# Deeper buffers between the engines of a selective scan, with its sums issued one step later

## The chip, the cores and the metric

The kernel runs on one core of a Trainium2 chip. A core has TensorE (PE), VectorE (DVE), ScalarE (ACT), GpSimd (POOL) and SyncE (SP); each takes its instructions in the order in which the program gives them to it, and waits at the head of its queue when an instruction needs something that is not there yet. SP's queue holds DMAs only. The metric is the device time of one execution in microseconds (us).

## The reference

Eight images of 64 channels by 64 x 64 go through four layers: attention over all 4096 positions with a depthwise convolution (layer 0), two blocks of window attention with MLPs (layer 1), a convolution by generated filters (layer 2), and a state-space layer (layer 3). The change concerns the scan of layer 3 most. Per image it has 128 channels, 16 states and four directions over the 4096 positions:

```
def step(h, inp):
    u_t, dt_t, B_t, C_t = inp
    h = h * jnp.exp(dt_t[..., None] * A) + dt_t[..., None] * B_t[:, :, None, :] * u_t[..., None]
    return (h, jnp.einsum('bkcn,bkn->bkc', h, C_t))
_, ys = jax.lax.scan(step, h0, (u, dt, Bl, Cl))
...
y = out_y[:, 0] + inv[:, 0] + wh + invwh
y = _ln(y, outnorm_g, outnorm_b, LN_EPS) * jax.nn.silu(z)
return jnp.einsum('bhwd,cd->bhwc', y, outproj_w) + outproj_b
```

Everything is float32.

## The kernel before

Images go in pairs, four pairs in all. For a pair, `front` does layers 0 to 2 and the inputs of layer 3, `scans` does the scan, and `back` the rest of layer 3. While the scans of pair p run, the back of pair p-1 and then the front of pair p+1 run beside them: `scans` takes a piece of that work (a Python generator that yields at each piece) after each scan step, as many as a fixed share of the whole asks for. In the last pair's scans there is only back work beside. The front of the first pair, with layer 0 of the second, comes ahead of all scans and takes about 2190 us.

A unit of the scan is one image, one direction and 512 positions; a pair has 64 units. A unit has eight steps, so there are 512 steps to a pair and 2048 in all. A step handles two states of all 128 channels: each partition holds one state of one channel, and the two halves of the channels lie side by side in tiles of 128 x 2 x 512.

A step i consists of these instructions:

- `fetch` (L1732): rows of B and of C are read from memory and spread over the partitions, by SP. B and C have four tiles each. B is fetched three steps ahead and C two.
- `products` (L1740): POOL multiplies B by dt times x, two steps ahead, into a tile `v`. There are six such tiles.
- `step`: ACT computes the two exponentials `dad` in PSUM (L1762), DVE scans (L1765) into a tile `h`, or into the PSUM tile itself, and ACT copies the last value of each scan to `carry` (L1773). Even steps have an `h` of two halves, odd steps of one, and there is one tile of each kind.
- The product with C overwrites `v`. `own` says how many of the two halves DVE multiplies (L1779) instead of POOL (L1776 for both halves, L1779 for one): 0 in even and 1 in odd steps, one more during the attention of layer 0, and 1, 1, 1, 2 in the last pair.
- `sums` (L1791): two matmuls with the constant matrix `fold` add the two states of each channel into the PSUM tile `yd`, which collects the eight steps of a unit. After the eighth, DVE adds `yd` into `Y` (L1803, L1805 or, for the fourth direction, L1808 into the tile `xs`, which SP stores as `ys`).

`inputs` prepares the unit after the next one: SP loads `xs` (L1705, two tiles), PE and ACT compute dt from it (L1708 to L1716), and SP spreads it over the partitions as `du` (L1719) and writes the rows of B and C to memory (L1725). The loop of `scans` writes all this in this order:

```
self.fetch(i + 3, steps[i + 3], 0)
self.fetch(i + 2, steps[i + 2], 1)
self.products(i + 2, steps[i + 2])
self.step(i, steps[i])
if i:
    self.sums(i - 1, steps[i - 1], steps[i]["w"])
while done < cost * (i + 1) / (n - LEAD):
    done += next(beside, cost)
if i % 8 == 1: self.inputs(self.units[i // 8 + 1])
```

A scheduler then puts each engine's instructions in order by its own estimate of when they are ready, so that several products can stand ahead of their step. `steps[i]["w"]` is the first product with C of step i; the sum is kept behind it in that estimate, which adds no wait on the chip.

Large tiles of the work beside the scans are slabs of 128 x 4356 floats, of which there are three; smaller ones come from pools that each part opens for itself, `w1a` and `w1m` for window attention and the MLP, `w2` for layer 2, `w4` and `w5` for back.

Of the kernel before, what the change touches and what calls it, by code (L numbers as in the profile page):

```python
# [9 lines left out]
F32 = mybir.dt.float32  # L10
# [7 lines left out]
P = 128  # L18
CH = 512
# [3 lines left out]
TAPS = 9  # L23
DI, NST, RNK, KDIR = 128, 16, 4, 4
TD = 512
NTD = L // TD
LEAD = 24
AHEAD = 0.8
# [60 lines left out]
def _pack(w):  # L89
# [105 lines left out]
    put("drT", f["dtproj_w"].transpose(2, 0, 1))  # L195
    al = f["A_logs"].reshape(KDIR, 2, 64, NST // 2, 2)
    put("alogs", al.transpose(2, 4, 0, 3, 1).reshape(P, KDIR, NST))
    put("fold", np.repeat(eye, 2, axis=0))
    dtT = f["dtproj_w"].transpose(2, 0, 1)
# [960 lines left out]
class _Direct:  # L1160
# [66 lines left out]
    def img(t):  # L1227
        return t.rearrange("p (h w) -> p h w", w=64)

    def memory(self, name, shape=(P, L)):  # L1230
        return self.dram.tile(list(shape), F32, name=name, tag=name)
# [128 lines left out]
    def layer1(self, X):  # L1360
        nc, tc, w, net = self.nc, self.tc, self.w, self.net
        with tc.tile_pool(name="w1n", bufs=2) as wk:
            for c in range(NCH):
                x = X[:, c * CH : (c + 1) * CH]
                pc, sd = self.normed(wk, lambda pc: [(pc, x)], w["cen64"], w["avg64"], net.eps[:, 0:1])
                nc.vector.scalar_tensor_tensor(x, pc, w["pe_g"], sd, ALU.mult, ALU.mult)
                nc.scalar.activation(x, x, AF.Identity, bias=w["pe_b"])
                yield 6
        for i in range(2):
            with tc.tile_pool(name="w1a", bufs=2) as wk:  # L1370
                now = self.window_head(i, 0, X, wk)
                for wy in range(8):

                    def ahead(wy=wy):
                        return self.window_head(i, wy + 1, X, wk) if wy < 7 else None

                    now = yield from self.window_row(i, wy, X, now, ahead, wk)
            with tc.tile_pool(name="w1m", bufs=2) as wk:
                yield from self.mlp(i, X, wk)

    def window_head(self, i, wy, X, wk):
# [16 lines left out]
        nc.tensor.matmul(pq, lhsT=w[f"qw{i}"], rhs=H, start=True, stop=True)  # L1398
        qx = wk.tile([P, 8, 4, 64], F32, name="w_qx", tag="w_qx", bufs=1)
        for s in range(4):  # L1400
# [21 lines left out]
    def window_row(self, i, wy, X, now, ahead, wk):  # L1422
# [6 lines left out]
        def scores(x):  # L1429

            es = []
            ss = [self.bank(f"w_s{g}", (P, 2, 4, 64)) for g in range(2)]
            for j in range(2):
                for g in range(2):
                    for im in range(2):
                        rows = slice(64 * im + 32 * g, 64 * im + 32 * g + 32)
                        nc.tensor.matmul(  # L1437
                            ss[g][half[im], j],
                            lhsT=K[rows, 64 * (x + j) : 64 * (x + j) + 64],
                            rhs=qx[rows, x + j],  # L1440
                            start=True,
                            stop=True,
                        )
            kinds = [2 * (wy == 7) + (x + j == 7) if shift else 0 for j in range(2)]
            for g in range(2):
                hs = slice(4 * g, 4 * g + 4)
                e = wk.tile([P, 2, 4, 64], F32, name="w_e", tag="w_e", bufs=4)
                b = bias[:, 0, hs].unsqueeze(1).to_broadcast([P, 2, 4, 64])
                nc.vector.tensor_tensor(e, ss[g], b, ALU.add)  # L1449
                for j in range(2):  # L1450
                    if kinds[j]:
                        m = net.smask[:, kinds[j] : kinds[j] + 1].to_broadcast([P, 4, 64])
                        nc.vector.tensor_tensor(e[:, j], e[:, j], m, ALU.add)
                nc.scalar.activation(e, e, AF.Exp)  # L1454
                es.append(e)
            return es
# [61 lines left out]
    def mlp(self, i, X, wk):  # L1518
        nc, w, net, half = self.nc, self.w, self.net, self.HALF
        gelus = []  # L1520
        for c in range(NCH):
            x = X[:, c * CH : (c + 1) * CH]
            pc, sd = self.normed(wk, lambda pc: [(pc, x)], w["cen64"], w["avg64"], net.eps[:, 0:1])
            H = wk.tile([P, CH], F32, name="m_h", tag="m_h")
            nc.vector.scalar_tensor_tensor(H, pc, w[f"norm2_g{i}"], sd, ALU.mult, ALU.mult)
            hid = []
            for im in range(2):
                ph = self.bank("ph")
                nc.tensor.matmul(ph, lhsT=w[f"f1w{i}"][half[im], :], rhs=H[half[im]], start=True, stop=True)
                h = wk.tile([P, CH], F32, name="hid", tag="hid", bufs=4)  # L1530
                g = nc.scalar.activation(h, ph, AF.Gelu, bias=net.bf1[:, i : i + 1])
                hid.append(h)
# [7 lines left out]
    def layer2(self, X):  # L1540
        nc, tc, w, net = self.nc, self.tc, self.w, self.net
        XP = self.padded("XP")
        for c in range(NCH):
            nc.scalar.activation(self.rows(XP, c), self.img(X[:, c * CH : (c + 1) * CH]), AF.Copy)
            yield 1
        nr = 2 * TAPS
        with tc.tile_pool(name="w2", bufs=2) as wk:
            net.load(wk, (5,))
            cf = net.channel_filters(X, wk, self.pf, "f")
            for c in range(NCH):  # L1550
# [18 lines left out]
                for t in range(TAPS):  # L1569
# [89 lines left out]
    def scans(self, p, beside, cost):  # L1659
# [16 lines left out]
        for i in range(-3, n):  # L1676
# [22 lines left out]
    def inputs(self, u):  # L1699
# [9 lines left out]
        one = wk.tile([P, 2, TD], F32, name="du1", tag="du1", bufs=1)  # L1709
        du = u["du"] = wk.tile([P, 2, 2, TD], F32, name="du", tag="du")  # L1710
        nc.scalar.activation(
# [4 lines left out]
        nc.scalar.activation(one[:, 0], pd, AF.Copy)  # L1716
        for g in range(2):
            src = one[self.HALF[g]].rearrange("c q t -> c (q t)").unsqueeze(1).to_broadcast([64, 2, 2 * TD])
            nc.sync.dma_start(du[:, g].rearrange("p q t -> p (q t)"), src)  # L1719
# [18 lines left out]
    def products(self, i, st):  # L1738
        v = st["v"] = self.sw.tile([P, 2, TD], F32, name="vd", tag="v", bufs=6)
        self.nc.gpsimd.tensor_tensor(v, self.twice(st["B"]), self.units[i // 8]["du"][:, :, 1], ALU.mult)  # L1740

    def step(self, i, st):
# [13 lines left out]

        h = wk.tile([P, 2 - i % 2, TD], F32, name="hd", tag=f"h{i % 2}", bufs=1)
        hs = []
# [53 lines left out]
    def back(self, p):  # L1812
        nc, tc, w, net, half = self.nc, self.tc, self.w, self.net, self.HALF
        out = net.out[2 * p : 2 * p + 2].rearrange("b c h w -> (b c) (h w)")
        X = self.flat("X3")
        F = self.padded("F")
        with tc.tile_pool(name="w4", bufs=2) as wk:
            for c in reversed(range(NCH)):
# [19 lines left out]
                yield 6  # L1838
        big = self.flat("big")
        with tc.tile_pool(name="w5", bufs=1) as wk:  # L1840
            prev, n, ups = F, 64, []
            for i in range(1, 4):
                n //= 2
                if i == 1:
                    hf = big[:, 0:2048].rearrange("p (a b) -> p a b", b=n)
                else:
                    hf = wk.tile([P, 2 * n, n], F32, name=f"half{i}", tag=f"half{i}")
                body = prev[:, 1 : 2 * n + 1, 1 : 2 * n + 1].rearrange("p h (w two) -> p h two w", two=2)
# [4 lines left out]
                nc.vector.tensor_tensor(pool[:, 1 : n + 1, 1 : n + 1], h2[:, :, 0, :], h2[:, :, 1, :], ALU.max)  # L1853
                cv = wk.tile([P, n, n], F32, name=f"cv{i}", tag=f"cv{i}")
                net.dwconv(cv, pool, w["mw"][:, i, :], w["mb"][:, i : i + 1], n)
                k = 2**i
                if i == 1:
                    up = big[:, 2048:4096].rearrange("p (a b) -> p a b", b=64)
                else:
                    up = wk.tile([P, n, 64], F32, name=f"up{i}", tag=f"up{i}")  # L1860
                nc.scalar.activation(
# [103 lines left out]
```

## Time and profile before

| | us |
|---|---|
| median of three runs (13265.84 to 13293.01) | 13285.64 |
| the profiled execution | 13288.26 |
| its span | 13286.5 |
| PE busy | 10111.5 (76%) |
| DVE busy | 8619.6 (65%) |
| POOL busy | 7760.7 (58%) |
| ACT busy | 7086.1 (53%) |

Busy time is the time in which an engine executes. The profile also names, for idle time of an engine, the instruction that came after it and what ended the wait. A line such as "PE yd L1791 <- POOL vd L1776: 996.9, 357, 22.3" says that PE was idle 996.9 us in all, 357 times, 22.3 us at the longest, ahead of the matmuls of line 1791 that write `yd`, until POOL's instruction of line 1776 ended. In a table of stretches, each engine's busy time and its count of instructions are given, then PEclk, the share of PE's full clock that was granted, the share of time in which the DMA engines were busy, and GB/s. A float32 matmul appears as two records.

### The profile page before, as it was taken

The numbers are of one execution on the slowest core, as the hardware profiler recorded it, in microseconds if no ns is written. First come the engines' busy times: TensorE is split into PE (matmuls) and PEld (weight loads), VectorE is DVE, ScalarE is ACT, GpSimd is POOL, SyncE is SP. The second block draws the span as 40 slices with busy tenths as digits, with TensorE's granted clock in tenths as the row PEclk, the third lists the DMA queues.
The fourth block names the chain that finished last, engine by engine and source line by source line (L and its number), as shares of the span: only waits on it lengthen the run. The fifth ranks groups of instructions, "written<-read, shape, count | busy, mean of one in ns | idle before, by whom it ended". The sixth has DMA issues, their size and how long they took to land. (4 is left out here: it accounts for less than half of the span.)

```text
span 13286.5 us, 142109 instructions
## 1 busy us (share of the span) xinstructions
PE 10111.5 (76%) x46358; PEld 3219.0 (24%) x46358; DVE 8619.6 (65%) x10109; ACT 7086.1 (53%) x15584; POOL 7760.7 (58%) x3875
## 2 busy tenths in 40 slices
PE   9999985777777567987888655997887756665566
PEld 2243421323221112223332111222432211111111
DVE  0121235777777676567676778557666777998997
ACT  5556514565545645665563644665555554554553
POOL 0000003888788684456675677447566777887994
PEclk9999976777787578998888676998788867777787
DMA  0000003444445553333343454334333455665663
GB/s 25 1 1 1 1 14 112 147 151 142 140 150 153 163 161 95 101 117 118 113 122 105 157 160 136 103 101 128 104 112 110 130 168 165 182 183 166 204 201 115
DMA packets 779986, 1579.99 MB, mean 119 GB/s; under 512 B 89312, under 2 KB 89440, under 8 KB 778208
## 3 DMA queue, kind: packets, MB, share of 16 engines
q1 hardware_dynamic: 755040, 1514.49, 37.9%
q10 hardware_dynamic: 24192, 56.32, 1.1%
q8 instruction: 367, 6.01, 0.2%
q14 instruction: 387, 3.17, 0.1%
HBM read 1199.26 MB, written 102.76 MB: 98 GB/s over the span
## 5 line engine op out<-in xcount | busy, mean ns | idle before, releaser
L1740 POOL TENSOR_TENSOR vd<-B,du 128x1024 f32<-128x1024 f32 x2048 | 4818.1, 2366 | 3533.2 <-DMA B<-rows 2362.5
L1791 PE MATMUL yd<-vd,pack 128*64 128x512 f32 x8192 | 3311.3, 782 | 1888.0 <-POOL vd L1776 996.9
L1762 ACT ACTIVATE dad<-du,As 128x512 f32<-128x512 f32 x4096 | 2722.3, 681 | 1059.7 <-DVE hd L1765 658.5
L1765 DVE TENSOR_TENSOR_SCAN hd<-dad,carry,vd 128x512 f32<-128x512 f32 x2166 | 2718.5, 1271 | 702.2 <-ACT dad L1762 412.7
L1776 POOL TENSOR_TENSOR vd<-hd,C 128x1024 f32<-128x1024 f32 x658 | 1553.8, 2361 | 1249.7 <-DVE hd L1765 1034.3
L1765 DVE TENSOR_TENSOR_SCAN dad<-dad,carry,vd 128x512 f32<-128x512 f32 x1418 | 1786.4, 1274 | 90.5 <-ACT dad L1762 66.6
L1779 POOL TENSOR_TENSOR vd<-hd,C 128x512 f32<-128x512 f32 x1154 | 1484.0, 1287 | 600.4 <-DVE hd L1765 564.6
L1791 PEld LDWEIGHTS yd<-vd,pack 128*64 128x64 f32 x8192 | 661.3, 162 | 4084.1 <-POOL vd L1776 1472.5
L1315 ACT ACTIVATE e<-s 128x512 f32<-128x512 f32 x2048 | 1201.0, 591 | 824.9 <-PE s L1309 821.3
L1309 PE MATMUL s<-X 64*128 64x512 f32 x4096 | 1337.4, 645 | 32.3 <-ACT e L1315 24.1
L1301 PE MATMUL po<-e,VT 128*64 128x512 f32 x4096 | 1200.0, 621 | 5.0 <-ACT e L1315 5.0
L1779 DVE TENSOR_TENSOR vd<-dad,C 128x512 f32<-128x512 f32 x1626 | 1078.5, 676 | 49.4 <-ACT carry L1773 47.2
L1773 ACT ACTIVATE carry<-hd 128x1 f32<-128x1 f32 (+1 forms) x1586 | 313.2, 200 | 785.7 <-DVE hd L1765 776.1
L1464 PEld LDWEIGHTS w_av<-vals,w_e 64*64 64x64 f32 x16384 | 614.3, 159 | 240.2 <-issue 110.4
L1464 PE MATMUL w_av<-vals,w_e 64*64 64x9 f32 x16384 | 643.4, 216 | 24.6 <-ACT w_e L1454 24.4
L1773 ACT ACTIVATE carry<-dad 128x1 f32<-128x1 f32 x1422 | 239.6, 169 | 701.9 <-DVE dad L1765 698.8
L1708 PE MATMUL pdd<-xs,xdt 128*128 128x512 f32 x512 | 397.0, 867 | 276.2 <-DMA xs<-xc 101.6
L1449 DVE TENSOR_TENSOR w_e<-w_s,bias 128x512 f32<-128x512 f32 x512 | 330.3, 682 | 417.4 <-PE w_s L1437 417.3
L1309 PEld LDWEIGHTS s<-X 64*128 64x128 f32 x4096 | 368.6, 186 | 925.1 <-issue 785.2
L1454 ACT ACTIVATE w_e<-w_e 128x512 f32<-128x512 f32 x512 | 310.2, 625 | 336.1 <-DVE w_e L1449 226.0
L1765 DVE TENSOR_TENSOR_SCAN hd<-dad,vd 128x512 f32<-128x512 f32 x304 | 362.8, 1212 | 168.6 <-POOL vd L1776 67.8
L1576 PE MATMUL acc<-tap,pack 128*128 128x512 f32 x576 | 381.4, 787 | 91.7 <-DVE tap L1575 89.4
(247 smaller groups left out, 10857.0 us busy)
## 6 DMA issues: line engine op xcount, KB each, us to landing
B<-rows SPq DMA_DIRECT2D x2048, 256.0 KB, 3.5
C<-rows SPq DMA_DIRECT2D x2048, 256.0 KB, 3.4
du<-du SPq DMA_DIRECT2D x512, 512.0 KB, 6.1
xs<-xt SPq DMA_DIRECT2D x128, 256.0 KB, 3.2
xs<-xc SPq DMA_DIRECT2D x128, 256.0 KB, 3.2
xc<-xcv ACTq DMA_DIRECT2D x64, 256.0 KB, 2.6
zs<-z ACTq DMA_DIRECT2D x64, 256.0 KB, 3.1
xt<-XT ACTq DMA_DIRECT2D x32, 512.0 KB, 5.0
```

What stands on the lines that cost most here:

```text
L1301: nc.tensor.matmul(po[half[im]], lhsT=VT[:, t, half[im]], rhs=es[im], start=(t == 0), stop=(t == 31))
L1309: nc.tensor.matmul(ss[im], lhsT=at(half[im], t), rhs=X[half[im], jc * CH : (jc + 1) * CH], start=True, stop=True)
L1315: nc.scalar.activation(e, ss[im], AF.Exp, scale=C**-0.5, accum_out=parts[:, im, t, jc : jc + 1])
L1464: nc.tensor.matmul(self.av[half[im], x % 4 + j, h, :], lhsT=es[h // 4][half[im], j, h % 4, :], rhs=V[half[im], x + j, h, :], start=True, s ...
L1708: nc.tensor.matmul(pd, lhsT=net.xdt[:, k, :], rhs=x, start=True, stop=True)
L1740: self.nc.gpsimd.tensor_tensor(v, self.twice(st["B"]), self.units[i // 8]["du"][:, :, 1], ALU.mult)
L1762: nc.scalar.activation(da, u["du"][:, j, 0], AF.Exp, scale=net.As[:, k, n : n + 1])
L1765: nc.vector.tensor_tensor_scan(along(to), along(da), along(v[:, j]), first, ALU.mult, ALU.add)
L1773: nc.scalar.activation(cs, ends, AF.Copy)
L1776: st["w"] = nc.gpsimd.tensor_tensor(v, h, self.twice(CC), ALU.mult)
L1779: m = engine.tensor_tensor(v[:, j], hs[j], CC, ALU.mult)
L1791: m = nc.tensor.matmul(u["y"][self.HALF[j]], lhsT=w["fold"], rhs=st["v"][:, j], start=(i % 8 == 0), stop=(i % 8 == 7))
```

## The change

The products get eight tiles `v` instead of six, and each kind of `h` two instead of one. The sums of step i-2, no longer those of step i-1, are issued after step i; the last two steps' sums come after the loop.

To have room, tiles of the work beside are laid into slabs. In layer 1 a slab `wide` takes the place of `w_qx`, the four `w_e`, the two `m_h` and the four `hid`. In layer 2 a slab `taps` holds four taps, where there were three, and the two `act`, whose zero borders are now written once for an image pair; `q2` goes from two tiles to one. In back, the slab `big` is taken at the start and first holds two `y` and two `z`, and later the half-pooled images and all three `up`. The number 2 of states to a step is also given a name, `GRP`.

```diff
+    def share(t, n):
+        return t[:, CH * n : CH * n + CH]
...
+        self.wide = self.flat("wide")
         for i in range(2):
+            self.nth = 0
...
-        qx = wk.tile([P, 8, 4, 64], F32, name="w_qx", tag="w_qx", bufs=1)
+        qx = self.wide[:, 0:2048].rearrange("p (x s q) -> p x s q", x=8, s=4)
...
-                e = wk.tile([P, 2, 4, 64], F32, name="w_e", tag="w_e", bufs=4)
+                e = self.share(self.wide, 4 + self.nth % 4).rearrange("p (j h q) -> p j h q", j=2, h=4)
+                self.nth += 1
...
-            H = wk.tile([P, CH], F32, name="m_h", tag="m_h")
+            H = self.share(self.wide, c % 2)
...
-                h = wk.tile([P, CH], F32, name="hid", tag="hid", bufs=4)
+                h = self.share(self.wide, 4 + 2 * (c % 2) + im)
...
+        taps = self.flat("taps")
+        acts = [taps[:, 2048 + 576 * j : 2624 + 576 * j].rearrange("p (h w) -> p h w", w=72) for j in range(2)]
+        for a in acts:
+            nc.vector.memset(a[:, :, 0:4], 0.0)
+            nc.vector.memset(a[:, :, 68:72], 0.0)
...
-                q = wk.tile([P, CH], F32, name="q2", tag="q2")
+                q = wk.tile([P, CH], F32, name="q2", tag="q2", bufs=1)
...
-                    tap = wk.tile([P, 8, 64], F32, name="tap", tag="tap", bufs=3)
+                    tap = self.img(self.share(taps, (TAPS * c + t) % 4))
...
-                a = wk.tile([P, 8, 72], F32, name="act", tag="act")
-                nc.vector.memset(a[:, :, 0:4], 0.0)
-                nc.vector.memset(a[:, :, 68:72], 0.0)
+                a = acts[c % 2]
...
-                if i:
-                    self.sums(i - 1, steps[i - 1], steps[i]["w"])
+                if i > 1:
+                    self.sums(i - 2, steps[i - 2], steps[i]["w"])
...
-        self.sums(n - 1, steps[n - 1])
+        for i in (n - 2, n - 1):
+            self.sums(i, steps[i])
...
-        v = st["v"] = self.sw.tile([P, 2, TD], F32, name="vd", tag="v", bufs=6)
+        v = st["v"] = self.sw.tile([P, 2, TD], F32, name="vd", tag="v", bufs=8)
...
-        h = wk.tile([P, 2 - i % 2, TD], F32, name="hd", tag=f"h{i % 2}", bufs=1)
+        h = wk.tile([P, 2 - i % 2, TD], F32, name="hd", tag=f"h{i % 2}", bufs=2)
...
+        big = self.flat("big")
         with tc.tile_pool(name="w4", bufs=2) as wk:
...
-                    y = wk.tile([P, CH], F32, name="yb", tag="yb")
-                    z = wk.tile([P, CH], F32, name="zb", tag="zb")
+                    y = self.share(big, im)
+                    z = self.share(big, 2 + im)
...
-                    hf = wk.tile([P, 2 * n, n], F32, name=f"half{i}", tag=f"half{i}")
+                at = (0, 1024, 1536)[i - 1]
+                hf = big[:, at : at + 2 * n * n].rearrange("p (a b) -> p a b", b=n)
...
-                    up = wk.tile([P, n, 64], F32, name=f"up{i}", tag=f"up{i}")
+                at = (2048, 0, 1024)[i - 1]
+                up = big[:, at : at + 64 * n].rearrange("p (a b) -> p a b", b=64)
```

More of the change, by code (lines that the diff above doesn't have):

```diff
@@ L26 @@
 NTD = L // TD
+GRP = 2
 LEAD = 24
@@ L195, in _pack @@
     put("drT", f["dtproj_w"].transpose(2, 0, 1))
-    al = f["A_logs"].reshape(KDIR, 2, 64, NST // 2, 2)
+    al = f["A_logs"].reshape(KDIR, GRP, P // GRP, NST // GRP, GRP)
     put("alogs", al.transpose(2, 4, 0, 3, 1).reshape(P, KDIR, NST))
-    put("fold", np.repeat(eye, 2, axis=0))
+    put("fold", np.repeat(np.eye(P // GRP, dtype=np.float32), GRP, axis=0))
     dtT = f["dtproj_w"].transpose(2, 0, 1)
@@ L1228, in img @@
         return t.rearrange("p (h w) -> p h w", w=64)
+    @staticmethod
+    def share(t, n):
+        return t[:, CH * n : CH * n + CH]
     def memory(self, name, shape=(P, L)):
@@ L1709, in inputs @@
         one = wk.tile([P, 2, TD], F32, name="du1", tag="du1", bufs=1)
-        du = u["du"] = wk.tile([P, 2, 2, TD], F32, name="du", tag="du")
+        du = u["du"] = wk.tile([P, GRP, 2, TD], F32, name="du", tag="du")
         nc.scalar.activation(
@@ L1716, in inputs @@
         nc.scalar.activation(one[:, 0], pd, AF.Copy)
-        for g in range(2):
-            src = one[self.HALF[g]].rearrange("c q t -> c (q t)").unsqueeze(1).to_broadcast([64, 2, 2 * TD])
+        m = P // GRP
+        for g in range(GRP):
+            src = one[m * g : m * g + m].rearrange("c q t -> c (q t)").unsqueeze(1).to_broadcast([m, GRP, 2 * TD])
             nc.sync.dma_start(du[:, g].rearrange("p q t -> p (q t)"), src)
@@ L1838, in back @@
                 yield 6
-        big = self.flat("big")
         with tc.tile_pool(name="w5", bufs=1) as wk:
@@ L1843, in back @@
                 n //= 2
-                if i == 1:
-                    hf = big[:, 0:2048].rearrange("p (a b) -> p a b", b=n)
-                else:
-                    hf = wk.tile([P, 2 * n, n], F32, name=f"half{i}", tag=f"half{i}")
+                at = (0, 1024, 1536)[i - 1]
+                hf = big[:, at : at + 2 * n * n].rearrange("p (a b) -> p a b", b=n)
                 body = prev[:, 1 : 2 * n + 1, 1 : 2 * n + 1].rearrange("p h (w two) -> p h two w", two=2)
@@ L1853, in back @@
                 nc.vector.tensor_tensor(pool[:, 1 : n + 1, 1 : n + 1], h2[:, :, 0, :], h2[:, :, 1, :], ALU.max)
-                cv = wk.tile([P, n, n], F32, name=f"cv{i}", tag=f"cv{i}")
+                if i == 1:
+                    cv = big[:, 0:1024].rearrange("p (a b) -> p a b", b=n)
+                else:
+                    cv = wk.tile([P, n, n], F32, name=f"cv{i}", tag=f"cv{i}")
                 net.dwconv(cv, pool, w["mw"][:, i, :], w["mb"][:, i : i + 1], n)
                 k = 2**i
-                if i == 1:
-                    up = big[:, 2048:4096].rearrange("p (a b) -> p a b", b=64)
-                else:
-                    up = wk.tile([P, n, 64], F32, name=f"up{i}", tag=f"up{i}")
+                at = (2048, 0, 1024)[i - 1]
+                up = big[:, at : at + 64 * n].rearrange("p (a b) -> p a b", b=64)
                 nc.scalar.activation(
```

## The prediction

> **What bounds the kernel now.** I began with the table of busy time by stage. Stages are cut where the kind of work in front of the scans changes. From 2190 us on, scan steps run without a break.
>
> ```profile
> core 0: us, PE busy (x) PEld busy (x) DVE busy (x) ACT busy (x) POOL busy (x), PEclk, DMA share, GB/s
> 2190.00:3200.00 1010.00, 786.36 (x5606) 309.95 (x5605) 735.20 (x843) 563.58 (x1140) 869.53 (x425) 0.77 0.50 150
> ...
> 5100.00:6000.00 900.00, 834.15 (x2882) 233.00 (x2882) 504.21 (x561) 569.89 (x1618) 422.49 (x211) 0.95 0.36 107
> ...
> 7200.00:8150.00 950.00, 563.42 (x1140) 136.02 (x1140) 711.20 (x752) 481.89 (x895) 690.24 (x336) 0.70 0.49 150
> ...
> 11000.00:13286.00 2286.00, 1374.23 (x2774) 296.02 (x2773) 2033.10 (x2228) 1144.06 (x2549) 1789.47 (x951) 0.78 0.58 174
> ```
>
> No engine is full in most of it. In the first stage PE is busy 78%, DVE 73%, POOL 86%; at 7200 it is 59, 75 and 73%. Two stages are different. During the attention of layer 0 (5100 to 6000, and again near 8150 to 9250) PE is busy 93%. In the last 2286 us DVE is busy 89%. So outside these, the queues wait for one another, and I asked PE's waits, then DVE's and POOL's, all from 2190 us to the end.
>
> ```profile
> PE yd L1791 <- POOL vd L1776: 996.9, 357, 22.3
> PE yd L1791 <- POOL vd L1779: 570.8, 282, 6.5
> PE yd L1791 <- DVE vd L1779: 186.9, 180, 5.6
> ...
> DVE Y L1805 <- PE yd L1791: 369.8, 72, 16.3
> DVE du L1715 <- ACT pdd L1714: 353.6, 139, 13.8
> DVE hd L1765 <- POOL vd L1776: 250.0, 162, 5.9
> ...
> POOL vd L1776 <- DVE hd L1765: 1034.3, 209, 37.7
> POOL vd L1740 <- PE yd L1791: 674.6, 220, 29.9
> ```
>
> The first three say that PE stood 1755 us at the head of its queue in front of a sum, since the product with C was not done. Added up by stage (all waits in front of yd), that is 557 us in 2190 to 5100, 333 in 6000 to 8150, 189 in 9250 to 11000, 687 in the last stage, and only 34 in the attention stage at 5100. In the first stage PE's 786 us of work and 173 us of such waits fill 95% of the time: PE's queue, not PE, is what is full there. The timeline shows one such place:
>
> ```profile
> 4425.50 2.34 POOL L1776 TENSOR_TENSOR vd<-hd,C 128x1024 f32<-128x1024 f32 x1
> ...
> 4427.88 1.28 DVE L1765 TENSOR_TENSOR_SCAN hd<-dad,carry,vd 128x512 f32<-128x512 f32 x1 [2.10 <-POOL vd L1776]
> ...
> 4427.90 1.98 PE L1791 MATMUL yd<-vd,pack 128*64 128x512 f32 x4 [0.94 <-POOL vd L1776]
> ```
>
> One product on POOL ends at 4427.84. DVE (2.10 us, because the only h tile of even steps was still being read) and PE (0.94 us) start 0.04 and 0.06 us later. These are the two waits that the change aims at.
>
> **What the Trainium skill says.** "PSUM — Partial Sum Buffer", section "Engine vs sequencer instructions": the queues of ScalarE, VectorE and GpSimd are strict FIFO and matmuls start in program order, so work for the next images behind a waiting sum is held too; the lines above agree. "Perfetto Trace Analysis", section "Optimization Strategy": a gap that repeats can mean that there are too few buffers; here it names a tile with one buffer. "TensorE: Matmul & The Clock Gate", section "What's actually happening": PE's clock is throttled by default and activity releases it. The trace agrees: granted 0.95 where PE is busy 93%, 0.70 where it is busy 59%. Fewer holes on PE should therefore not cost clock, and may gain some; I price that at zero. "SBUF — State Buffer", section "Who interferes with whom": a DVE instruction with at most one SBUF input does not contend with GpSimd. The scans read one operand from PSUM, and POOL's products show 2327 ns at least and 2353 ns in the median, so more overlap of the two should not lengthen them.
>
> **The change part by part.**
>
> *Sums two steps later.* Counts stay (4096 fold matmuls, each shown as two records). In the two programs' orders on PE, two matmuls, one step, fewer stand in front of any given piece of front work in the median; the place has moved as it says. A sum then has a whole step (5.0 us in the first scan, 6.3 in the second and third, 3.9 in the last) between product and use. The median wait from the end of a product to its sum is 1.1 us in the first scan and 0.05 in the last, so one step covers nearly all of the 1755 us on PE itself. What is late next is POOL (86%) or DVE (73%). Bounds: zero, if PE's holes cost nothing, or all 557 + 333 + 189 = 1079 us outside attention and the last stage. I take one third, 360 us: POOL needs 2.37 + (2.36 + 1.29) / 2 = 4.2 us per step against 4.75 in the first stage (425 products in 1010 us, two a step), which alone lets at most 12% go there, and each of several queues that are full to three quarters will take over a part. In the attention stages I take nothing, because PE's own work fills them.
>
> *Two h tiles of each kind.* It takes away DVE's waits on L1776 and L1779 as readers of h: 250.0 + 34.4 = 284 us. These overlap with the gain above (when POOL is late, PE and DVE both wait), so they are not added to it. In the last stage, where DVE's idle time is 2286 - 2033 = 253 us, I take 40 us for both edits. Bounds 0 and 253.
>
> *Eight product tiles.* Product i+8 now needs sum i, which stands one step later, so POOL gains one step, not two. On POOL's queue three products on average stood between step i's product with B and its product with C; now it is 3.6, five at most instead of four. About half of POOL's wait for PE (675 us) lies in attention (162 us in 5200 to 5900, 185 in 8200 to 9200), where PE is full, and is worth nothing by itself. The products are early anyway, 12 us in the median ahead of their scan in the first scan. Taken as zero, from -100 to +150 (second rival).
>
> *The last sum of a unit.* The add into Y waits for it on DVE (369.8 + 101.2 + 24.1 = 495 us, 310 of it in or around attention), with the scans of the next step queued behind, and for half of the units the load of xs waits for that add, with B's and C's fetches behind it on SP; one unit in four also stores ys from it. In DVE's order the add stands after the fourth scan of the next unit before and after, so the load doesn't move, but the sum stands closer to the add. Bounds: -330 us, if two thirds of the wait go with PE's holes, to +256 x 1.3 = +330 us if each add waits out one more record pair. I take zero.
>
> *Tiles in slabs.* The depth stays: w_qx one, w_e four, hid four, m_h two, y and z two each; taps go from three to four, q2 from two to one (the next square comes a whole chunk of nine taps later, when PE has read it). The slab for back is asked for before its loads, when the front's last slab has been drained. Cover: nothing waits for these in the lines above; without it a few us for each of four images' pairs. 48 memsets of 85 ns fewer on DVE (-4 us), two table loads of 1283 ns more on ACT (+3 us): zero.
>
> Sum: -360 - 40 = -400 us. The profiled execution took 13288 us (span 13286.5), the median of the three runs is 13286, so they can stand for each other: 13288 - 400 = 12888, say 12890.
>
> **The rivals.**
>
> *The holes were free (no change, 13285 us).* PE is busy only 60 to 80%, and what PE loses in front of a sum it makes up before DVE notices. For it: POOL's product with C itself waits 1034 us for DVE's scans, so the ring closes over DVE and POOL. Against it: DVE's own waits on PE come to 1308 us, its largest class, and on POOL to 405.
>
> *POOL runs too far ahead (slower, 13450 us).* B and C still have four tiles. With five products ahead, the fetch of a unit's first B stands in SP's queue behind a fetch of C whose tile a product with C must free; in POOL's new order only one instruction (2.36 us) lies between that product and the one that needs the B in 82 of 255 units, against 5 before. A fetch of B takes 3.5 us to land and 0.5 to issue, as does the C ahead of it, so each shows about 2 us: 82 x 2 = 164 us, with products with C, then sums, queued behind. Unit by unit POOL already idles there (178 us on B during the scans). It decides when these holes come to more than what PE and DVE recover; with a recovery near zero the sum is 13288 + 164. Against it: POOL has 14% to 35% to spare, and the sums behind it now have a step of slack.
>
> *More than a third comes back (12610 us).* If half of the 1079 us and half of the 284 go, 540 + 142 = 682 us are gained; POOL would then have to run at over 90% in the first stages.
>
> That the order doesn't move is excluded by the orders themselves.
>
> **How the numbers follow.** A gain of about a third 0.58, more than that 0.18, no change 0.07, slower 0.17. Range: from 12560, a little under the third rival, to 13400, which leaves out the worse half of the slower case. 0.2% is about what a measurement of this kernel can tell from no change: faster by more 0.76, within it 0.07, slower by more 0.17.
>
> **What would show it.** Right: PE's waits in front of yd fall from 1755 to under 600 us, DVE's waits on L1776 and L1779 to under 60, POOL's share in the first stage rises to 90% or more, and steps there take about 4.6 us. The attention stages and the last one keep their length. Wrong: PE's waits fall but DVE's waits on ACT (1251 us) or POOL's on B grow by as much; or DVE's wait for the sum at the add into Y grows over 700 us.

## The result, and the profile after

| | before | changed kernel |
|---|---|---|
| median of 20 runs | 13287.98 us | 13297.76 us |
| the profiled execution, its span | 13288.26, 13286.5 us | 13298.23, 13296.3 us |
| PE's waits in front of `yd`, from 2190 us on | 1755 us | 1194 us |
| PE's waits in front of `pdd` | 274 us | 717 us |
| time in which DVE isn't busy, from 2190 us on | 2988 us | 3006 us |

The ratio is 1.001, with a 95% interval of 1.0003 to 1.0018: no change within the 0.2% named in the prediction, where 12890 us were forecast. Line numbers shift: in the changed kernel the products with B are L1753, the scans L1778, the products with C L1789 (both halves) and L1792 (one), the sums L1804, the additions into `Y` L1816 and L1818, the loads of `xs` L1717, and dt's matmul `pdd` L1720. In the kernels of the experiments they shift again by a few lines.

First the table of busy time by stage, with the columns of the table before (after each stretch its length, then busy us and instructions of PE, PE's weight loads, DVE, ACT and POOL).

```profile
2190.00:3200.00 1010.00, 772.01 (x5960) 314.54 (x5960) 771.32 (x887) 584.78 (x1187) 905.89 (x442) 0.78 0.51 155
...
5100.00:6000.00 900.00, 818.81 (x2828) 218.47 (x2826) 516.62 (x571) 568.00 (x1627) 451.06 (x225) 0.95 0.35 106
...
7200.00:8150.00 950.00, 525.26 (x1049) 126.33 (x1048) 727.19 (x787) 495.41 (x914) 700.53 (x337) 0.67 0.49 151
...
11000.00:13296.00 2296.00, 1236.82 (x2592) 275.62 (x2590) 1939.55 (x2130) 1093.70 (x2426) 1669.80 (x895) 0.72 0.54 163
```

In the first stage POOL did 442 products where it did 425, so steps came 4% faster. In the attention stage PE is full as before. From the trace, the last pair's scan begins at 11000 us instead of 11145: the first three scans gained 145 us. The last one lost 155: it takes 2296 us to the end, not 2141, and DVE is busy 84% of it, where it was busy 90% of those 2141 us. A gain and a loss stand behind "no change". PE's waits from 2190 us on name the loss. First those for the load of `xs` in the kernel before, then the longest in the changed kernel:

```profile
PE pdd L1708 <- DMA xs<-xc: 101.6, 24, 8.2
...
PE pdd L1708 <- DMA xs<-xt: 57.5, 33, 5.7
```

```profile
PE yd L1804 <- POOL vd L1792: 592.9, 256, 8.5
PE yd L1804 <- POOL vd L1789: 497.4, 164, 11.3
PE pdd L1720 <- DMA xs<-xc: 271.1, 36, 17.0
PE pdd L1720 <- DMA xs<-xt: 222.1, 38, 17.6
...
PE yd L1804 <- DVE vd L1792: 104.1, 98, 3.7
```

The waits of `yd` fell by a third. In their place PE waits 493 us for the load of `xs`, where it waited 159. In the last pair's scan alone that is 227 us against 73. DVE's waits show where this goes on:

```profile
DVE Y L1818 <- PE yd L1804: 505.6, 91, 22.0
DVE du L1727 <- ACT pdd L1726: 501.1, 149, 22.1
DVE hd L1778 <- ACT dad L1775: 375.2, 188, 12.1
...
DVE Y L1816 <- PE yd L1804: 112.6, 30, 29.8
```

`du` waits 501 us for ACT instead of 354, and ACT waits 743 us for `pdd` instead of 476. The scans wait 22 us for readers of `h`, where it was 284. The timeline shows the boundary of two units in the last scan (start, duration, engine and line; in brackets the idle time before and what ended it):

```profile
12276.98 1.06 DVE L1816 SCALAR_TENSOR_TENSOR Y<-xs,dsum,yd 128x512 f32<-128x512 f32 x1
...
12278.07 0.33 SPq L1717 DMA_DIRECT2D xs<-xt  x1
...
12281.00 2.05 PE L1720 MATMUL pdd<-xs,xdt 128*128 128x512 f32 x2 [8.73 <-DMA xs<-xt]
...
12287.62 0.65 ACT L1723 ACTIVATE pdd<-pdd,pack 128x512 f32<-128x512 f32 x1
...
12292.49 0.54 SPq L1738 DMA_DIRECT2D rows<-bc  x1
...
12295.21 1.41 SPq L1745 DMA_DIRECT2D B<-rows  x1
```

`inputs` runs in the second step of a unit and prepares the unit that follows. Seen from the unit whose last sum has just been issued, that is the unit after next, and since there are two `xs` tiles, its load takes over the tile of the unit just summed. Here the add into `Y` is the last reader of that tile. The load is issued 0.03 us after the add and lands 2.9 us later. On PE, `pdd` stands directly behind the last sum of the unit, so PE does nothing for 8.73 us between: 4.7 us until the add has its turn on DVE, which is busy with scans and products in front of it, 1.1 us for the add, and 2.9 us for the load. After that come dt on ACT, the rows of B in memory, and the first B of the next unit 17 us after the add.

In the order on PE, the two fold matmuls of one step of the next unit stood between the last sum and `pdd` in the median before, and none stand there now: the sum moved a step down, and `pdd` did not. That step was the slack of the `xs` load. The load itself came later too. In the 112 units in which the trace shows it behind an add that uses its tile, it was issued on average 13.0 us after the first scan of the next unit before and 16.2 us now in the first three pairs, and 7.7 and 11.6 us in the last pair.

A second change is on POOL's queue. Counted in the programs' orders, 3.59 products with B stand there on average between a step's product with B and its product with C, where it was 3.01 ("products ahead" from here on). What that does is seen at 7548 us:

```profile
7548.15 6.96 POOL L1753 TENSOR_TENSOR vd<-B,du 128x1024 f32<-128x1024 f32 x3
...
7548.23 0.20 ACT L1786 ACTIVATE carry<-hd 128x2 f32<-128x2 f32 x1 [0.68 <-DVE hd L1778]
...
7555.07 2.34 POOL L1789 TENSOR_TENSOR vd<-hd,C 128x1024 f32<-128x1024 f32 x1
...
7557.47 1.12 PE L1804 MATMUL yd<-vd,pack 128*64 128x512 f32 x2 [5.86 <-POOL vd L1789]
```

The scan is done at 7548.20 (ACT copies its ends at once), but POOL first works off three products with B, and PE stands 5.86 us for the product with C. Over the whole execution I added up, for each of the 1812 products with C on POOL, the time from the end of its scan in which POOL worked on products with B: 2270 us before, 4141 us now.

### The profile page after: what moved, and what is told of

Same layout as the page of the kernel before. It is cut to its first block, busy times and chain, and to the rows that moved or that the text cites. A ratio compares the mean times of both kernels' runs of the same rounds, so it can differ in the third digit from the quotient of the medians.

```text
span 13296.3 us, 141895 instructions
## 1 busy us (share of the span) xinstructions
PE 9888.9 (74%) x46358; PEld 3202.5 (24%) x46358; DVE 8611.2 (65%) x10061; ACT 7088.8 (53%) x15586; POOL 7761.8 (58%) x3875
## 5 line engine op out<-in xcount | busy, mean ns | idle before, releaser
L1753 POOL TENSOR_TENSOR vd<-B,du 128x1024 f32<-128x1024 f32 x2048 | 4818.1, 2370 | 3317.2 <-DMA B<-rows 2453.7
L1804 PE MATMUL yd<-vd,pack 128*64 128x512 f32 x8192 | 3042.6, 768 | 1248.7 <-POOL vd L1792 592.9
L1778 DVE TENSOR_TENSOR_SCAN hd<-dad,carry,vd 128x512 f32<-128x512 f32 x2166 | 2709.0, 1270 | 415.9 <-ACT dad L1775 334.8
L1789 POOL TENSOR_TENSOR vd<-hd,C 128x1024 f32<-128x1024 f32 x658 | 1556.3, 2365 | 1254.5 <-DVE hd L1778 836.1
L1792 POOL TENSOR_TENSOR vd<-hd,C 128x512 f32<-128x512 f32 x1154 | 1479.4, 1284 | 821.0 <-DVE hd L1778 794.5
L1778 DVE TENSOR_TENSOR_SCAN dad<-dad,carry,vd 128x512 f32<-128x512 f32 x1418 | 1788.5, 1275 | 63.3 <-ACT dad L1775 47.5
L1804 PEld LDWEIGHTS yd<-vd,pack 128*64 128x64 f32 x8192 | 655.1, 162 | 3243.5 <-POOL vd L1792 1104.0
L1792 DVE TENSOR_TENSOR vd<-dad,C 128x512 f32<-128x512 f32 x1626 | 1080.6, 677 | 121.4 <-ACT carry L1786 74.1
L1720 PE MATMUL pdd<-xs,xdt 128*128 128x512 f32 x512 | 432.0, 939 | 718.8 <-DMA xs<-xc 271.1
L1472 PE MATMUL w_av<-vals,wide 64*64 64x9 f32 x16384 | 621.4, 212 | 63.6 <-ACT wide L1462 63.0
L1472 PEld LDWEIGHTS w_av<-vals,wide 64*64 64x64 f32 x16384 | 592.5, 154 | 253.7 <-ACT wide L1462 116.9
L1457 DVE TENSOR_TENSOR wide<-w_s,bias 128x512 f32<-128x512 f32 x512 | 331.6, 683 | 413.7 <-PE w_s L1444 405.9
L1723 ACT ACTIVATE pdd<-pdd,pack 128x512 f32<-128x512 f32 x256 | 169.0, 660 | 746.0 <-PE pdd L1720 745.7
L1462 ACT ACTIVATE wide<-wide 128x512 f32<-128x512 f32 x512 | 312.0, 626 | 389.6 <-DVE wide L1457 248.5
L1727 DVE TENSOR_TENSOR du<-pdd,xs 128x512 f32<-128x512 f32 x256 | 175.8, 687 | 504.6 <-ACT pdd L1726 504.5
```

Of the source, the lines that this page charges most:

```text
L1472: nc.tensor.matmul(self.av[half[im], x % 4 + j, h, :], lhsT=es[h // 4][half[im], j, h % 4, :], rhs=V[half[im], x + j, h, :], start=True, s ...
L1720: nc.tensor.matmul(pd, lhsT=net.xdt[:, k, :], rhs=x, start=True, stop=True)
L1778: nc.vector.tensor_tensor_scan(along(to), along(da), along(v[:, j]), first, ALU.mult, ALU.add)
L1789: st["w"] = nc.gpsimd.tensor_tensor(v, h, self.twice(CC), ALU.mult)
L1792: m = engine.tensor_tensor(v[:, j], hs[j], CC, ALU.mult)
L1804: m = nc.tensor.matmul(u["y"][self.HALF[j]], lhsT=w["fold"], rhs=st["v"][:, j], start=(i % 8 == 0), stop=(i % 8 == 7))
```

## The experiments

The expectations name theories by letters. At the start stood **the xs load** (A): the later sum brings the add, the load behind it and `pdd` later, and what PE gains in front of `yd` it loses in front of `pdd`. Its rivals were that the holes were free (B), that POOL runs too far ahead of the fetches of B (C), and that the slabs cost time. When e1_sum1 was slower than any of them had said, **POOL's order** (F) came up: eight tiles let more products with B stand ahead of the product with C. Its rivals were that the third `xs` tile is the whole gain (D), that eight tiles are needed (G), that the second `h` tiles do the harm, and that the later sum is worth nothing.

The runs fall into four sets, in which the median of the kernel before lay at 13279, 13280, 13286 and 13268 us. So between runs of different sets I read nothing into differences of 20 us or less. Diffs are against the changed kernel. Of the pieces that come back in several kernels, "sums one step later" means

```diff
-                if i > 1:
-                    self.sums(i - 2, steps[i - 2], steps[i]["w"])
+                if i:
+                    self.sums(i - 1, steps[i - 1], steps[i]["w"])
...
-        for i in (n - 2, n - 1):
-            self.sums(i, steps[i])
+        self.sums(n - 1, steps[n - 1])
```

**Sums one step later as before, the rest of the change kept (e1_sum1).** The piece above alone.

> The changed kernel with the sums back at one step after their own (eight product tiles, two h tiles of each kind, the slabs kept). Theory A (the later sums give with one hand and take with the other: they free PE from waiting for POOL, but the add into Y, the load of xs behind it and pdd behind that come later): PE's waits in front of yd go back from 1194 to about 1700 us, its idle time before pdd from 719 to about 280 us, DVE stays free of the 284 us of waits for readers of h, and the time is a little under the kernel before, 13150 to 13290 us. Theory B (the holes were free, deeper buffers and later sums move nothing): within 0.2% of 13288. Theory C (POOL runs too far ahead of the fetches of B, because of eight tiles): slower than before or equal, 13290 to 13450, with POOL's wait on B still near 270 us.

Measured: 13510.13 us, ratio to before 1.0165 (1.0142 to 1.0187). That is slower than all three theories had it. So the rest of the change, without the later sums, costs 1.65%. PE's waits in front of `yd` for POOL are 2055 us (1571 before), and products with C lie behind products with B for 4212 us. The waits for `xs` are 159 us, as before: their growth to 493 us comes with the later sums.

**A third `xs` tile (e2_xs3).**

```diff
-        x = u["x"] = wk.tile([P, TD], F32, name="xs", tag="xs")
+        x = u["x"] = wk.tile([P, TD], F32, name="xs", tag="xs", bufs=3)
```

> The changed kernel with three xs tiles instead of two, so that the load of xs for the unit after next waits for no add into Y. Theory A: PE's wait in pdd for DMAs of xs falls from 493 us to under 150, the last 2296 us shrink to about 2140, and the whole takes 13000 to 13140 us (-1.2 to -2.2%). Theory B: PE's waits may fall, the time stays within 0.3% of 13290. Theory C: POOL's wait on B is as before, time stays at 13290.

Measured: 12850.22 us, ratio 0.9667 (0.9644 to 0.9690), 448 us less than the changed kernel. PE's waits of `pdd` for the load, from 2190 us on:

```profile
PE pdd L1720 <- DMA xs<-xc: 8.2, 5, 2.3
...
PE pdd L1720 <- DMA xs<-xt: 7.2, 4, 3.4
```

493 us have become 15, and `du`'s wait for ACT on DVE went from 501 to 120. The edit takes away only what the load waits for, but the scheduler's order follows it: of the 248 `pdd` that come behind a sum in the program, 129 now stand in front of that sum on PE, where 66 did in the changed kernel. Either way the chain starts earlier, and the first theory holds. The gain is larger than the 160 to 300 us that it forecast.

**One step in the last pair, two elsewhere (e11_split).**

```diff
-                if i > 1:
-                    self.sums(i - 2, steps[i - 2], steps[i]["w"])
+                lag = 1 if p == B // 2 - 1 else 2
+                if i >= lag:
+                    self.sums(i - lag, steps[i - lag], steps[i]["w"])
...
-        for i in (n - 2, n - 1):
+        for i in range(n - (1 if p == B // 2 - 1 else 2), n):
             self.sums(i, steps[i])
```

> The changed kernel, with the sums one step after their own in the last pair's scans and two steps in the first three. In the changed kernel the last scan starts 145 us earlier than in the kernel before and takes 155 us longer. Theory A: the gain of the first three stays and the loss of the last goes: 13110 to 13170 us. Theory B and C: the two differences are not from the sums' place, so the time stays at 13270 to 13310.

Measured: 13242.37 us, ratio 0.9975 (0.9962 to 0.9989). The last pair's scan began at 10993 us, so the gain of the first three stayed, but it still took 2230 us to the end, against 2141 before and 2296 in the changed kernel. So 66 of the 155 us lost there go with the later sums, less than theory A had it. The rest goes with the product tiles: with six tiles and sums one step later (e9_slabs_h2 below), the last pair's scan took 2144 us.

**The slabs alone (e4_slabs).** Sums one step later, and

```diff
-        v = ... tag="v", bufs=8)
+        v = ... tag="v", bufs=6)
...
-        h = ... tag=f"h{i % 2}", bufs=2)
+        h = ... tag=f"h{i % 2}", bufs=1)
```

> The slabs alone: six product tiles, one h tile of each kind and sums one step later as in the kernel before, but the tiles of the work beside laid into slabs. All theories: within 0.3% of 13288 us. If the slabs cost something by themselves, it shows here as 13330 us or more, and the gain of the rest was hidden by it.

Measured: 13299.88 us, ratio 1.0010 (0.9996 to 1.0023). The slabs cost nothing that can be told.

**Slabs and second `h` tiles (e9_slabs_h2).** As e4_slabs, with `bufs=2` kept for `h`.

> The second h tile alone: slabs, six product tiles, two h tiles of each kind, sums one step after their own. With eight product tiles this took 13510 us. Theory F: the harm is of the product tiles, so this is at 13100 to 13300 us and DVE's 284 us of waits for readers of h are gone. Rival: the second h tile lets DVE run ahead of POOL and does the harm, 13400 to 13520 us.

Measured: 13250.27 us, ratio 0.9977 (0.9967 to 0.9987). The 284 us of waits for readers of `h` fell to 10, for 50 us of time against e4_slabs. With e1_sum1, which differs in the tiles alone, it says that two more product tiles cost 260 us there.

**All of the change but for the product tiles (e6_v6).** `bufs=6` for `v` alone.

> The changed kernel with six product tiles instead of eight (two xs tiles as in the changed kernel). Theory F: faster than the changed kernel's 13298, 13050 to 13200 us, PE's waits in front of yd under 800 us instead of 1194, with pdd's wait for xs still above 400 us. Theory G: slower, 13320 to 13500 us.

Measured: 13271.39 us, ratio 0.9988 (0.9975 to 1.0001), which neither theory had. Beside e9_slabs_h2, the later sums alone are worth nothing here (+21 us): the waits of `yd` for POOL fall from 1632 to 828 us, those for `xs` rise from 162 to 406, and the scans' waits for products with B from 161 to 351.

**The slabs with a third `xs` tile (e14_slabs_xs3), then a second `h` too (e17_sum1_v6_h2_xs3), then the later sums too (e15_v6_xs3).** Each is the kernel of e4, e9 and e6 with `bufs=3` for `xs`.

> The third xs tile alone: slabs, six product tiles, one h tile of each kind, sums one step after their own, three xs tiles. With all parts of the change and three xs tiles the kernel took 12850 us. Theory A (the change is worth 3% and the xs chain took it away): most of the 12850 needs the change, so this takes 13130 to 13260 us. Theory D (the third xs tile is the whole gain and the change is worth nothing with or without it): 12800 to 12900 us.

> Three xs tiles, six product tiles, two h tiles of each kind, sums one step after their own: against the 12760 us of the same with the sums two steps later, this is what the later sums are worth when xs is not in the way. Theory A: PE's waits in front of yd are near 1600 us again instead of 821, and the time is 12900 to 12990 us. Rival (the later sums are worth nothing, the second h tile gave the difference to 12997): 12730 to 12800 us.

> The changed kernel with three xs tiles and only six product tiles. In the order of the program 2.4 products stand on POOL between a step's product with B and its product with C, against 3.7 with eight tiles and three xs. Theory F (eight tiles do harm, since products with B get ahead of the product with C that a sum waits for): 12600 to 12800 us, less than the 12850 of eight tiles, and PE's waits in front of yd fall from 1316 to under 800 us. Theory G (eight tiles are needed, because the later sums hold a tile one step longer): 12900 to 13150 us with POOL's wait for PE growing over 929 us.

Measured: 12997.07 us, ratio 0.9787 (0.9757 to 0.9816); 12925.32 us, 0.9735 (0.9719 to 0.9751); 12759.89 us, 0.9605 (0.9577 to 0.9633). The third tile gives 303 us with no other part of the change but the slabs, so the load of `xs` held up the kernel before as well; neither theory had this size for e14. With it and six product tiles, the later sums are worth 165 us.

**Eight product tiles with sums one step later and three `xs` tiles (e8_sum1_xs3).**

> Three xs tiles, eight product tiles, two h tiles of each kind, sums one step after their own. Theory F (eight tiles put products with B ahead of the product with C on POOL, 4.1 on average instead of 3.1): slower than the same with six tiles by 100 us or more, 13050 to 13250 us, with PE's waits in front of yd over 1800 us. Rival (the 13510 us with two xs tiles came from the xs chain alone): within 60 us of the same with six tiles.

Measured: 13228.12 us, ratio 0.9955 (0.9941 to 0.9969). Against e17, two more tiles cost 303 us. Against e2, the later sums are worth 378 us with eight tiles; but they change POOL's order as well there, from 4.06 products ahead to 3.66.

**Seven product tiles, later sums and three `xs` tiles (e18_v7_xs3).**

> The changed kernel with three xs tiles and seven product tiles: 3.05 products ahead on POOL, between 2.4 with six tiles (12760 us) and 3.7 with eight (12850 us). Theory F: the time follows the products ahead, 12780 to 12830 us, and PE's waits in front of yd lie between 821 and 1266 us. Rival (there is a best number, since with six tiles DVE's scans wait 361 us for products with B): under 12740 us.

Measured: 12712.59 us, ratio 0.9571 (0.9555 to 0.9587), less than with six (12760) and with eight (12850): the rival held, and not theory F. The scans wait 361 us for products with B with six tiles, 287 with seven and 186 with eight; the products with C lie behind products with B for 3270, 3953 and 5020 us. The number of tiles trades one for the other, and neither sum can be read as time lost.

**The inputs asked for one step later (e7_late).** This gives `pdd` its distance back, with two `xs` tiles.

```diff
-            if i % 8 == 1 and i // 8 + 1 < len(self.units):
+            if i % 8 == 2 and i // 8 + 1 < len(self.units):
```

> The changed kernel with the inputs of the next unit issued one step later (after the third step of a unit, not the second), two xs tiles as in the changed kernel. Theory A (pdd stands too close behind the add into Y): in the program's order one more sum stands between them, so PE's wait in pdd for xs falls from 493 to under 250 us and the time to 13100 to 13230 us. Rival (the load itself is late, wherever pdd stands): the wait only moves on to du and the rows of B and C, POOL's wait on B rises over 500 us and the time is 13300 us or more.

Measured: 13409.01 us, ratio 1.0087 (1.0070 to 1.0104). PE's wait for `xs` falls only to 311 us, and POOL's waits for DMAs, without the one in front of its first product, rise from 424 to 653 us, 521 of them for B. This is what the rival had said. The chain from `xs` to the first B of a unit has no step to give; a third tile (e2_xs3) lets it start earlier.

**Eight tiles in the order of six, and of seven (e20_sum1_xs3_order6, e21_xs3_order7).** They are e8 and e2 with each product with B kept behind an earlier sum in the scheduler's estimate, which adds no wait on the chip:

```diff
+        self.summed = {}
...
-        self.nc.gpsimd.tensor_tensor(v, self.twice(st["B"]), ...)
+        m = self.nc.gpsimd.tensor_tensor(v, self.twice(st["B"]), ...)
+        if i >= 7:                                     # 6 in e20
+            self.net.behind(m, self.summed[i - 7])     # 6 in e20
...
             if after is not None and j == 0:
                 net.behind(m, after)
+        self.summed[i] = m
```

> Sums one step later as before, eight product tiles, two h, three xs tiles, and each product with B kept behind the sum six steps earlier in the scheduler's estimate only, so that POOL's queue is laid out almost as with six tiles (3.10 products with B on average between a step's product with B and its product with C; 4.06 without this, 3.08 with six tiles) while eight tiles remain. Theory that the order on POOL's queue does the harm of eight tiles: the time of six tiles, 12925 +- 50 us. Rival, that the tiles do it by themselves (where they lie, or what they let DVE and ACT do): it stays at the 13228 us of eight tiles, +- 50.

> Sums two steps later, eight product tiles, two h, three xs tiles, and each product with B kept behind the sum seven steps earlier in the scheduler's estimate only (3.07 products ahead on average; 3.66 without this, 3.05 with seven tiles). Theory of the order: the 12713 us of seven tiles, +- 40, or a little less, since a product with B that the estimate puts too late for seven tiles finds a tile free. Rival, the tiles by themselves: the 12850 us of eight tiles.

Measured: 12828.87 us, ratio 0.9665 (0.9647 to 0.9684), and 12673.45 us, ratio 0.9541 (0.9522 to 0.9560). With the order alone, e8's 13228 us fall by 399, and e2's 12850 by 177. Products with C lie behind products with B for 2699 us (4706 in e8) and 3894 us (5020 in e2). PE's waits from 2190 us on, of e8 first and then of e20 (products with C are L1788 for both halves and L1791 for one in e8, and L1791 and L1794 in e20):

```profile
PE yd L1803 <- POOL vd L1788: 1221.8, 376, 15.4
PE yd L1803 <- POOL vd L1791: 777.6, 303, 9.6
```

```profile
PE yd L1806 <- POOL vd L1791: 937.8, 322, 9.2
PE yd L1806 <- POOL vd L1794: 570.1, 302, 7.4
```

So the order on POOL's queue is the cause, and the tiles by themselves are not. I had expected the time of six and seven tiles; both came out lower, by 96 us against e17 and 39 against e18. With the order held, two more tiles (e20) and one more (e21) are a small gain. The kernel e21 is the fastest of all, 4.6% under the kernel before. Its first and last stages (the last pair's scan begins at 10586 us there, so the second row starts some way into it):

```profile
2190.00:3200.00 1010.00, 804.98 (x6401) 331.16 (x6400) 836.72 (x953) 621.11 (x1268) 967.51 (x473) 0.79 0.54 166
11000.00:12650.00 1650.00, 966.68 (x2067) 213.75 (x2068) 1559.71 (x1727) 860.08 (x1901) 1310.42 (x700) 0.74 0.59 178
```

POOL is busy 96% of the first stage with 473 products in it, 4.27 us a step, close to the 4.2 us of work a step that the prediction worked out: here POOL is nearly full. DVE is at 95% in the last stage.

## Why the prediction was wrong, point by point

The runs that add one part at a time lay the change out in its own terms. Down the table parts are added, across it the third `xs` tile; with sums one step later, eight product tiles took 13510 (e1) and 13228 us (e8).

| medians, us | two `xs` tiles | three `xs` tiles |
|---|---|---|
| slabs | 13300 (e4) | 12997 (e14) |
| and two `h` tiles | 13250 (e9) | 12925 (e17) |
| and sums two steps later | 13271 (e6) | 12760 (e15) |
| and eight product tiles | 13298 (the change) | 12850 (e2) |
| and seven tiles' order | not run | 12673 (e21) |

*"The last sum of a unit … I take zero" is the step whose mechanism failed.* The prediction saw that "for half of the units the load of xs waits for that add" and that the sum comes to stand closer to it, but reasoned from DVE's order: the add stays after the fourth scan, "so the load doesn't move". It did move: against the first scan of the next unit it was issued 3 to 4 us later, and with the later sums alone (e6 against e9) 2.3 us later. In the last pair the add had stood behind the third scan (27 of 30 such units) and now stood behind the fourth (25 of 30). And the prediction didn't ask what stands between the last sum and `pdd` on PE. That slack went to nothing, and `pdd`'s waits grew by 443 us. With six product tiles, the later sums are worth 165 us with a third `xs` tile and -21 with two, so this term took 186 us; with eight it took 166 (378 and 212). It lay within the bounds of ±330 us that the prediction gave. That the load takes the gain away is shown; how much of it comes from the lost slack and how much from the later load is not, since e7 moves both. "The Trainium skill", page "Perfetto Trace Analysis", section "Optimization Strategy", says to find what blocks a gap and make that dependency start sooner, the source code showing the dataflow. The runs agree: starting the load sooner, by a third tile, took 448 us off, while moving the waiting instruction (e7) made the kernel slower. The wait showed before the change as 159 us and was worth 303 us when removed (e4 to e14). More than PE waited on it: DVE's waits for ACT fell from 1296 to 860 us in the same step.

*"Sums two steps later", -360 us, is the step that was too large.* A third of 1079 us was a guess at what other queues would take over. Even with the load out of the way the later sums are worth 165 us with six tiles, and 155 us between e20 and e21, where the products ahead are nearly the same (3.10 and 3.07). Which queue takes up how much of the rest is not settled. The waits of `yd` did fall, from 1755 to 1194 us, and not to the 600 that were to show the forecast right.

*"Eight product tiles … Taken as zero, from -100 to +150" hid the order on POOL.* They cost 27 us in the change itself (e6 against it) and 90 with a third `xs` tile, inside the bounds, but 260 (e9 to e1) and 303 us (e17 to e8) with sums one step later. So it is the later sums that repay most of their harm, and neither part can be priced alone. The prediction counted "3.6, five at most instead of four" products in between, and then used only what POOL gains from tiles that come free. It did not price what those places cost the product with C behind them: up to 2.36 us each, for PE, and through `h` for DVE.

Sums and tiles together changed the time by +48 us (e9 to the change), where -360 were forecast. One way to divide the 408 us between: 195 are the size of the sums' term, 123 the load (with a third `xs` tile the two parts give -75, e17 to e2), and 90 the tiles.

*"Two h tiles", with -40 us for both edits in the last stage, was nearly right* in size: 50 us (e4 to e9) and 72 (e14 to e17), while the 284 us of waits fell to 22, as said. But the gain doesn't lie in the last stage, where it was expected: the last pair's scan took 2138 us in e4 and 2144 in e9. So the size was luck. *"Slabs", zero, was right* (e4). In the first stage the signs of being right came: POOL is busy 90%, and a step takes 4.6 us.

*Of the rivals,* "the holes were free" gave the right time by a wrong mechanism: PE's holes are worth 165 us, but were paid for elsewhere. "POOL runs too far ahead" named the right queue, but the wrong victim. It expected B to be late, by 164 us, and POOL's waits for B grew only from 178 to 272 us; the product with C was late. Of the signs of error, none came: DVE's wait for the sum at the add into `Y` is 654 us in all, up from 495 and under 700, and DVE's waits for ACT and POOL's for B grew by 94 us each, not by the 561 us that PE's waits fell. What took their place stood on PE's own queue, in front of `pdd`.

## What to carry to other kernels

When an instruction is moved down an in-order queue, list not only what gets slack, but what stood right behind it and now stands right against it, and follow the buffer that its result frees; a wait that is already there with a few us at each turn can be the next bound. More buffers for a producer are also permission for the scheduler to place it further ahead: count what then stands in front of its consumer on the same queue, and if that grows, hold the order and keep the buffers. Take parts of such a change one at a time, and in more than one order, since here gains and losses cancelled to 0.1%, and what one part was worth hung on the other.

## What the runs showed of the hardware

Nothing unexpected. Two costs that the prediction set at zero held under more overlap: in e21 the mean scan of the commonest form takes 1272 ns and the mean product with B 2372 ns, against 1271 and 2366 ns before, in 4.6% less time. (The page that the prediction cites for this, "SBUF — State Buffer", section "Who interferes with whom", has a condition that the prediction left out, "outside the 2-port perf modes"; no run here bears on it.) PE's granted clock was 0.817 before, 0.810 in the changed kernel and 0.828 in e21. It went with PE's idle time from 2190 us on, 2994, 3226 and 2800 us: the fewer holes that the prediction counted on came in e21, not in the changed kernel.
